# Order of the loads and of the closing products in a LoRA-conditioned routed feed-forward kernel

## The chip, the cores and the metric

The kernel runs on one core of one Trainium2 chip. The metric is the device time of one execution in microseconds, the median of several runs. All data are float32.

## What is computed

Cut to what matters, the reference is this (SCALING of the first part is 2, of the second 1; E is 8 experts, R is 16):

```python
base = einsum('bti,oi->bto', x, W) + b                      # x: 8 x 512 x 2048, W: 2048 x 2048
lora = einsum('btr,bro->bto', einsum('bti,bir->btr', x, lora_As[itok]), lora_Bs[itok])
c = base + 2 * lora                                         # never needed in full
logits = einsum('bsd,ed->bse', c, route_w)                  # 8 logits per token
top, e = top_k(logits, 1)                                   # one expert per token
h = einsum('bsd,erd->bser', c, A)                           # 8 x 16 head values per token
out = x + einsum('bser,eor->bso', one_hot(e) * top * h, Bw)
```

The token's 128 head values and 8 logits are linear in c, and c is linear in x. So the kernel never forms c: it first multiplies W into the 136 columns of A and route_w ("folds" W), and then each tile of 128 tokens needs one product with the folded matrix, a small correction for bias and adapters, the choice of the expert, and one product with Bw.

## The kernel before

**First stage, folding.** W is read in 16 chunks of 128 rows (`load_w`, 1 MB each, four buffers), and `proj`, the 136 columns of A and route_w, in pieces (`load_pj`, tile `pj`, 16 chunks of 68 KB). `chunk_w(oc)` copies chunk `oc` into a layout that TensorE can use as weights, half on ScalarE and half on VectorE (L286, tiles `wv`, two buffers for each half), and issues the load of chunk `oc + 4` into the buffer that comes free. `fold_w(oc)` multiplies it into six PSUM banks `pc` (L297); after the last chunk each bank is copied into `cm`, the folded matrix (L307), by ScalarE and VectorE in turn. Each float32 product is two instructions on TensorE. Between the folds lie the smaller jobs: the indirect loads of the batch's adapters on GpSimd's queue (L173, L203), transposing them (`turn_adapters`, `turn(ad_aT, ...)`), the bias (`fold_bias`, `project_bias`, whose result goes to `g4`), and `project_adapters`, whose result goes through DRAM (`g_dram`) back into `g4`. Before all this GpSimd loads `it_i`, the eight adapter numbers, to every partition (L92).

**Second stage, tokens.** There are 32 tiles `t` of 128 tokens; two tiles are one x unit of 2 MB (`load_x(u)`, L123). To have x with its columns on the partitions, a unit is first moved in 16 blocks of 32 x 1024 (`shuffle`, L254, on GpSimd and ScalarE, tile `xq`), and then VectorE transposes within blocks (`turn_x`, L239, tile `xT`). The main loop takes half a tile per step `n`:

- `heads(t, j0, j1)`, L409: products of xT with `cm` into the PSUM bank `ph`;
- `turn_low(t)`, L421 and L428, on VectorE: the 16 adapter values of the tile, spread and transposed into `hT`; then `add_low(t)`, L433, adds their product with `g4` to `ph`;
- `route(t)`, L446 to L454, on VectorE: five small operations that choose the expert and leave the weighted head values `wh`;
- `turn_heads(t)`, L464, transposes `wh` on TensorE into `pw`, `keep_heads(t)`, L469, copies it to `whT` on ScalarE;
- `delta(t, h)`, L479: the product of whT with 1024 columns of `fb` (Bw) into two banks `po`; `add_delta(t, h)`, L499, adds it to x in place on VectorE, and `store`, L510, writes the result.

`piece(n)` says which half tile is at its `delta` in step n: three steps after its heads. The tiles are written in the order in which each engine shall work (a hand-made order, `manual_schedule`); each engine takes its instructions in that order, and waits stand only where data or buffers ask for them. The queue of SyncE (SP) issues almost all loads and stores. [...]two in `ps_s`, six in `ps_c` for the fold, which afterwards become two in `ps_h` (for `ph`) and four in `ps_o` (for `po`).

The order at the very start, on SP's queue but for the first line:

```python
load_pj(0, 1, nc.scalar)
load_w(0)
load_pj(1, 3)
load_w(1)
load_pj(3, 5)
```

Of the kernel before, what the change touches and what calls it, by code (L numbers as in the profile page):

```python
# [9 lines left out]
F32 = mybir.dt.float32  # L10
# [8 lines left out]
def kernel(  # L19
# [29 lines left out]
    nc = tc.nc  # L49
    P = 128  # L50
    Q = 32
    NQ = P // Q
    B, T, D = x.shape
# [4 lines left out]
    R = ER // E  # L58
    NJ = D // P
# [3 lines left out]
    NT = B * TPB  # L63
# [3 lines left out]
    HJ = NJ // 2  # L67
    HN = D // 512 // 2
    NA = NP + R
# [10 lines left out]
    ps_s = ctx.enter_context(tc.tile_pool(name="ps_s", bufs=2, space=bass.MemoryType.PSUM))  # L80
# [15 lines left out]
    def load_pj(c0, c1, eng=nc.sync):  # L96
        eng.dma_start(out=pj[:, c0:c1, :], in_=proj_v[:, c0:c1, :])
# [3 lines left out]
    def load_w(oc):  # L101
        wt = wpool.tile([P, D], F32, tag="w", bufs=4, name=f"w_{oc}")
        nc.sync.dma_start(out=wt, in_=w[ts(oc, P), :])  # L103
        w_tiles.append(wt)

    load_pj(0, 1, nc.scalar)
    load_w(0)
    load_pj(1, 3)
    load_w(1)
    load_pj(3, 5)  # L110
    load_w(2)
# [3 lines left out]
    x_tiles = {}  # L115
# [3 lines left out]
    def load_x(u):  # L119
        xt = xpools[u % XB].tile([P, TPU, D], F32, tag=f"x{u % XB}", name=f"x_{u}")  # L120
        for k in range(TPU):
            b, r = divmod(TPU * u + k, TPB)
            nc.sync.dma_start(out=xt[:, k, :], in_=x[b, ts(r, P), :])  # L123
        x_tiles[u] = xt
# [3 lines left out]
    make_identity(nc, ident)  # L128

    nc.scalar.copy(warm_a[:, 1:2], warm_a[:, :1])  # L130
    pm = ps_s.tile([P, P], F32, tag="s", name="pm")
    for _ in range(14):
        nc.tensor.matmul(pm, warm, warm, start=True, stop=True)
# [24 lines left out]
    fb = const.tile([P, D], F32, name="fb")  # L158
# [71 lines left out]
    cm = const.tile([P, NJ, NA + R], F32, name="cm")  # L230
    ad_aT = const.tile([P, NJ, P], F32, name="ad_aT")
# [13 lines left out]
    moves = [(g, i) for i in range(NQ) for g in range(NQ)]  # L245

    def shuffle(u, ms, copy):

        if not ms:
            return  # L250
        if u not in xq_tiles:
            xq_tiles[u] = qpool.tile([P, TPU, NQ, DQ], F32, tag="q", name=f"xq_{u}")
        for g, i in ms:
            copy(xq_tiles[u][ts(i, Q), :, g, :], x_tiles[u][ts(g, Q), :, ts(i, DQ)])  # L254
# [66 lines left out]
    def turn_adapters(g):  # L321
        pt = ps_s.tile([P, 4, P], F32, tag="s", name=f"pbT_{g}")
        for k in range(4):
            nc.tensor.transpose(pt[:, k, :], ad_b[:, ts(4 * g + k, P)], ident)  # L324
        nc.scalar.copy(ad_bT[:, ts(g, 4), :], pt)
# [4 lines left out]
    def project_bias():  # L330

        pb = ps_s.tile([P, NP], F32, tag="s", name="pb")
        nc.tensor.matmul(
            pb, one.rearrange("p i s -> p (i s)"), bp, start=True, stop=True
        )
        nc.vector.tensor_copy(g4, pb.unsqueeze(1).to_broadcast([P, B, NP]))
# [16 lines left out]
    for oc in range(NO):  # L353
        if oc + 1 < NO:
            chunk_w(oc + 1)
        fold_w(oc)
        if oc == 2:
            fill_constants()
        if oc == 4:
            load_adapters_b()  # L360
        if oc == 7:
            load_adapters_a()
        if 8 <= oc < 12:
            turn_adapters(oc - 8)
        if oc in (9, 10):
            fold_bias(range(8 * (oc - 9), 8 * (oc - 8)))
        if oc == 10:
            load_x(0)
            nc.sync.dma_start(out=fb, in_=ffn_b)
            load_x(1)  # L370
            load_x(2)
        if oc in (10, 11):
            turn(ad_aT, ad_ar, oc - 10)
        if oc == 11:
            project_bias()
        if oc == 12:
            project_adapters()
            shuffle(0, moves[6:], nc.gpsimd.tensor_copy)
        if oc in (12, 13, 14):
            shuffle(0, moves[2 * (oc - 12) : 2 * (oc - 11)], nc.scalar.copy)  # L380
        if oc == 13:
            for b in range(2):
                nc.vector.tensor_copy(cm[:, :, ds(b * NA, R)], ad_aT[:, :, ts(b, R)])
        if oc == 14:
            for h in range(2):
                turn_x(0, h)
    wctx.close()
    ps_h = ctx.enter_context(tc.tile_pool(name="ps_h", bufs=2, space=bass.MemoryType.PSUM))
    ps_o = ctx.enter_context(tc.tile_pool(name="ps_o", bufs=2, space=bass.MemoryType.PSUM))
# [8 lines left out]
    whT_tiles = {}  # L398
    po_tiles = {}

    def batch_of(t):
        return t // TPB

    def heads(t, j0, j1):
        s = batch_of(t) % 2
        if j0 == 0:
            ph_tiles[t] = ps_h.tile([P, 512], F32, tag="h", name=f"ph_{t}")[:, :NA]
        for j in range(j0, j1):
            nc.tensor.matmul(  # L409
                ph_tiles[t],  # L410
                xT_tiles[t][:, j, :],
                cm[:, j, ds(s * R, NA)],
                start=(j == 0),
                stop=(j == NJ - 1),
            )
# [15 lines left out]
    def add_low(t):  # L431
        b = batch_of(t)
        nc.tensor.matmul(  # L433
            ph_tiles[t][:, ds((1 - b % 2) * R, NP)],
            hT_tiles.pop(t),
            g4[:, b, :],
            start=False,
            stop=True,
            skip_group_check=True,
        )  # L440
# [21 lines left out]
    def turn_heads(t):  # L462
        pw = ps_s.tile([P, P], F32, tag="s", name=f"pw_{t}")
        nc.tensor.transpose(pw, wh_tiles.pop(t), ident)  # L464
        pw_tiles[t] = pw
# [2 lines left out]
        whT_tiles[t] = small.tile([P, P], F32, tag="whT", name=f"whT_{t}")  # L468
        nc.scalar.copy(whT_tiles[t], pw_tiles.pop(t))  # L469

    def delta(t, h):

        if (t, h) == (NT - 1, 0):

            po = [ps_h.tile([P, 512], F32, tag="h", name=f"po_{t}_{k}") for k in range(HN)]
        else:
            po = ps_o.tile([P, HN, 512], F32, tag="o", name=f"po_{t}_{h}")
        for k in range(HN):
            nc.tensor.matmul(  # L479
                po[k] if isinstance(po, list) else po[:, k, :],  # L480
                whT_tiles[t],
                fb[:, ts(h * HN + k, 512)],
                start=True,
                stop=True,
            )
        po_tiles[t, h] = po

    def add_delta(t, h):
        u, k = divmod(t, TPU)
        po = po_tiles.pop((t, h))  # L490
        if t < NT - 1:
            parts = [po.rearrange("p n d -> p (n d)")]
        else:
            parts = po if isinstance(po, list) else [po[:, m, :] for m in range(HN)]
        n = D // 2 // len(parts)
        for m, part in enumerate(parts):
            cols = ds(h * D // 2 + m * n, n)
            xs = x_tiles[u][:, k, cols]
            nc.vector.tensor_tensor(xs, xs, part, ALU.add)  # L499
            if t == NT - 1:  # L500
                store(t, cols)
        if t == NT - 2:
            store(t, ts(h, D // 2))
        elif t < NT - 2 and h == 1:
            store(t, ds(0, D))

    def store(t, cols):
        u, k = divmod(t, TPU)
        b, r = divmod(t, TPB)
        nc.sync.dma_start(out=out[b, ts(r, P), cols], in_=x_tiles[u][:, k, cols])  # L510

    def piece(n):

        return divmod(n - 3, 2) if 0 <= n - 3 < 2 * NT else (-1, -1)
# [15 lines left out]
    for n in range(2 * NT + 4):  # L530
        t, h = divmod(n, 2)
        if t < NT:

            if n == 3:
                heads(t, HJ, HJ + HJ // 2)
                turn_heads(0)
                heads(t, HJ + HJ // 2, NJ)
            else:
                heads(t, h * HJ, (h + 1) * HJ)
            if n == 2:  # L540
                add_low(0)
        if h == 0 and 0 < t <= NT:
            route(t - 1)
        tp, hp = piece(n - 1)
        if tp >= 0:
            add_delta(tp, hp)
        turn_x(t + 1, h)
        if h == 1 and 0 < t <= NT:
            keep_heads(t - 1)
        u, ms = shuffle_slot(n)  # L550
        shuffle(u, ms, nc.gpsimd.tensor_copy if n == 2 else nc.scalar.copy)
        if h == 1 and t < NT:
            turn_low(t)
        if piece(n)[0] >= 0:
            delta(*piece(n))
        if h == 1 and 0 < t < NT:
            add_low(t)
        if h == 1 and t < NT:
            b, k = divmod(t, TPB)
            if k == 0 and 0 < b < B - 1:  # L560
                nc.gpsimd.tensor_copy(
                    cm[:, :, ds((b + 1) % 2 * NA, R)], ad_aT[:, :, ts(b + 1, R)]
                )
        if h == 0 and 1 < t <= NT:
            turn_heads(t - 1)
        tq, hq = piece(n - 5)
        u, k = divmod(tq, TPU)
        if tq >= 0 and hq == 1 and k == TPU - 1 and u + XB < NU:
            load_x(u + XB)
# [48 lines left out]
```

## Time and profile before

| | |
|---|---|
| median of 3 runs | 338.23 us (337.25 to 338.35) |
| profiled execution, its own time | 337.22 us |
| span of the profile | 335.4 us, granted TensorE clock 0.996 |
| PE busy | 324.5 us (97%) |
| DVE busy | 233.4 us (70%) |
| ACT busy | 171.1 us (51%) |
| POOL busy | 136.0 us (41%) |
| moved by DMA | 88.8 MB, 265 GB/s on average |

PE is TensorE's stream of matmuls, PEld its weight loads, DVE is VectorE, ACT ScalarE, POOL GpSimd, SP SyncE; a name with a q behind it is the engine's queue. Times in the profile count from the start of the span. A busy share is an average over the whole span; where the work of one engine fills 97% of it, what that engine waited for in the rest is found in its own timeline, in the brackets ahead of each group.

### The profile page before, as it was taken

How to read it: one execution, taken by the hardware profiler on the slowest of the kernel's cores; microseconds unless marked ns; L12 is line 12 of the kernel's file. 1: busy time of each engine (PE TensorE's matmuls, PEld its weight loads, DVE VectorE, ACT ScalarE, POOL GpSimd, SP SyncE). 2: the span in 40 equal slices, each digit the busy share in tenths (PEclk: the TensorE clock that was granted, in tenths of full speed). 3: DMA queues.
4: the chain of work that ended last, by engine and by line, in shares of the span. 5: the costliest groups of instructions: out<-in, count | busy, mean ns of one | idle time of the engine just before them, and what ended most of it. 6: DMA issues, size and time to landing. Idle time of an engine off the chain costs nothing.

```text
span 335.4 us, 5111 instructions
## 1 busy us (share of the span) xinstructions
PE 324.5 (97%) x1966; PEld 260.3 (78%) x1966; DVE 233.4 (70%) x424; ACT 171.1 (51%) x193; POOL 136.0 (41%) x143
## 2 busy tenths in 40 slices
PE   8899999978999999999999999999999999999993
PEld 8799999978777777777777777777777777777751
DVE  1132385555887877787878787877888777777754
ACT  3233133854857566576647565757575664830000
POOL 2001400899981807182616354344718080800000
PEclk9999999999999999999999999999999999999998
DMA  7999999959233394949485766758494949333336
GB/s 217 402 405 422 416 408 422 419 199 386 117 128 141 132 377 186 376 160 385 136 365 168 335 215 285 256 248 328 174 374 172 374 165 380 164 125 127 126 125 250
DMA packets 15655, 88.82 MB, mean 265 GB/s; under 512 B 1664, under 2 KB 4368, under 8 KB 5392
## 3 DMA queue, kind: packets, MB, share of 16 engines
q1 hardware_dynamic: 14960, 86.33, 65.5%
q0 software_dynamic: 528, 2.11, 2.0%
q8 instruction: 15, 0.25, 0.3%
q10 hardware_dynamic: 144, 0.07, 0.1%
q14 instruction: 8, 0.07, 0.1%
HBM read 54.88 MB, written 33.62 MB: 264 GB/s over the span
## 4 chain that ended last, share of the span: by engine, by line
PE 86%; DMA 6%; POOL 3%; DVE 2%; issue 1%; ACT 1%; SPq 0%; DVEq 0%; POOLq 0%; ACTq 0%
PE ph L409 39%; PE po L479 33%; PE pc L297 10%; DMA x<-in_x_dram 3%; POOL xq L254 3%; DMA w<-in_w_dram 3%; PE ph L433 2%; PE pw L464 1%; DVE xT L239 1%; ACT wv L286 1%; DVE cm L307 0%; PE pbT L324 0%; DVE rw L452 0%; SPq L103 0%; DVE x L499 0%
## 5 line engine op out<-in xcount | busy, mean ns | idle before, releaser
L254 POOL COPY xq<-x 32x1024 f32<-32x1024 f32 x121 | 125.9, 1041 | 122.6 <-DMA x<-in_x_dram 80.7
L254 ACT COPY xq<-x 32x1024 f32<-32x1024 f32 x135 | 140.8, 1043 | 23.8 <-DMA x<-in_x_dram 16.7
L409 PE MATMUL ph<-cm,xT 128*128 128x152 f32 x1024 | 142.7, 293 | 1.8 <-DVE cm L307 1.8
L409 PEld LDWEIGHTS ph<-cm,xT 128*128 128x128 f32 x1024 | 135.2, 190 | 10.6 <-issue 10.6
L479 PE MATMUL po<-fb,whT 128*128 128x512 f32 x256 | 120.2, 592 | 0.4 <-ACT whT L469 0.4
L499 DVE TENSOR_TENSOR x<-x,po 128x1024 f32<-128x1024 f32 (+1 forms) x66 | 77.5, 1178 | 6.6 <-PE po L479 6.2
L239 DVE STREAM_TRANSPOSE xT<-xq 128x1024 f32<-128x1024 f32 x64 | 78.8, 1234 | 4.2 <-POOL xq L254 4.2
L479 PEld LDWEIGHTS po<-fb,whT 128*128 128x128 f32 x256 | 44.8, 190 | 31.8 <-issue 30.9
L297 PE MATMUL pc<-pj,wv 128*128 128x136 f32 x512 | 60.7, 279 | 1.7 <-ACT wv L286 1.6
L297 PEld LDWEIGHTS pc<-pj,wv 128*128 128x128 f32 x512 | 59.8, 190 | 2.1 <-ACT wv L286 1.8
L469 ACT COPY whT<-pw 128x128 f32<-128x128 f32 x32 | 8.5, 266 | 89.7 <-PE pw L464 89.7
L446 DVE TENSOR_REDUCE top<-ph 128x1 f32<-128x8 f32 x32 | 5.3, 167 | 39.0 <-PE ph L433 39.0
L286 DVE COPY wv<-w 128x1024 f32<-128x1024 f32 (+1 forms) x17 | 12.6, 745 | 28.2 <-DMA w<-in_w_dram 16.5
L286 ACT COPY wv<-w 128x1024 f32<-128x1024 f32 (+1 forms) x17 | 16.8, 996 | 24.9 <-DMA w<-in_w_dram 23.4
L433 PEld LDWEIGHTS ph<-g,hT 128*128 128x128 f32 x64 | 12.1, 190 | 14.8 <-issue 12.6
L452 DVE TENSOR_SCALAR rw<-rank,win,top 128x8 f32<-128x8 f32 x32 | 15.6, 488 | 1.2
L433 PE MATMUL ph<-g,hT 128*128 128x136 f32 x64 | 12.6, 279 | 0.0
L464 PEld LDWEIGHTS pw<-ident,wh 128*128 128x128 f32 x32 | 4.5, 140 | 8.7 <-issue 5.7
L428 DVE STREAM_TRANSPOSE hT<-hls 128x128 f32<-128x128 f32 x32 | 10.0, 311 | 1.1
L173 POOL DMA_INDIRECT raw<-in_cond_b_dram,brow_i x1 | 1.0, 1031 | 23.5 <-DVE brow_i L172 23.5
L454 DVE TENSOR_TENSOR wh<-ph,rw 128x128 f32<-128x128 f32 x32 | 9.3, 292 | 1.1
L464 PE MATMUL pw<-ident,wh 128*128 128x128 f32 x32 | 8.8, 274 | 0.8 <-DVE wh L454 0.8
(61 smaller groups left out, 73.5 us busy)
## 6 DMA issues: line engine op xcount, KB each, us to landing
x<-in_x_dram SPq DMA_DIRECT2D x32, 1024.0 KB, 9.0
out_dram<-x SPq DMA_DIRECT2D x30, 1024.0 KB, 4.9
w<-in_w_dram SPq DMA_DIRECT2D x16, 1024.0 KB, 11.2
fb<-in_ffn_b_dram SPq DMA_DIRECT2D x1, 1024.0 KB, 13.1
out_dram<-x SPq DMA_DIRECT2D x2, 512.0 KB, 2.7
out_dram<-x SPq DMA_DIRECT2D x4, 256.0 KB, 2.9
pj<-in_proj_dram SPq DMA_DIRECT2D x2, 272.0 KB, 12.7
pj<-in_proj_dram SPq DMA_DIRECT2D x2, 136.0 KB, 8.0
```

The costliest lines, as they stand in the source:

```text
L239: nc.vector.transpose(dst[:, ts(h, HJ), :].rearrange("p j (g t) -> p g j t", t=Q), src.rearrange("p g (j a) -> p g j a", a=Q)[:, :, ts(h, ...
L254: copy(xq_tiles[u][ts(i, Q), :, g, :], x_tiles[u][ts(g, Q), :, ts(i, DQ)])
L286: copy(dst[:, ts(k, n)], wr[:, ds(h * HJ + k * n, n)])
L297: nc.tensor.matmul(pc[:, k, :], wv_tiles[oc, h][:, j, :], pj[:, oc, :], start=(oc == 0 and k == 0), stop=(oc == NO - 1), skip_group_check= ...
L409: nc.tensor.matmul(ph_tiles[t], xT_tiles[t][:, j, :], cm[:, j, ds(s * R, NA)], start=(j == 0), stop=(j == NJ - 1),)
L428: nc.vector.transpose(hT, h.rearrange("p g s -> p (g s)"))
L433: nc.tensor.matmul(ph_tiles[t][:, ds((1 - b % 2) * R, NP)], hT_tiles.pop(t), g4[:, b, :], start=False, stop=True, skip_group_check=True,)
L452: nc.vector.tensor_scalar(rw, rank, win, top, ALU.is_equal, ALU.mult)
L454: nc.vector.tensor_tensor(wh.rearrange("p (e r) -> p e r", r=R), ph[:, :ER].rearrange("p (e r) -> p e r", r=R), rw.unsqueeze(2).to_broadca ...
L464: nc.tensor.transpose(pw, wh_tiles.pop(t), ident)
L479: nc.tensor.matmul(po[k] if isinstance(po, list) else po[:, k, :], whT_tiles[t], fb[:, ts(h * HN + k, 512)], start=True, stop=True,)
L499: nc.vector.tensor_tensor(xs, xs, part, ALU.add)
```

## The change

Four edits, all of them of order and placing; the computation is the same.

- At the start, W's second chunk is issued directly behind the first on SP's queue. The piece of `proj` for chunks 1 and 2, which stood between them, is issued on ScalarE's queue, after ScalarE's first small copy.
- The first x unit is loaded after fold 8 instead of fold 10, which puts it ahead of the loads of the last two W chunks on SP's queue (14 and 15). Its ten GpSimd blocks are written right behind it. `fb` and x units 1 and 2 are issued one fold later in the text, behind the same W load as before. `project_bias` comes ahead of the second adapter transpose, and the two copies of adapters into `cm` (L383) after fold 11 instead of fold 13.
- In step 2, `add_low(0)` stands in the middle of the half tile's heads instead of behind them.
- In the last two steps that have a `delta` of tile 30, `add_low(31)` and `turn_heads(31)` go in between the two products of that delta. The last tile's results lie in separate banks: two of 512 columns for its first half, and 512, 256 and 256 for the second, each with its own add and its own store; every second store of that tile is issued on ScalarE's queue.

```diff
     load_pj(0, 1, nc.scalar)
     load_w(0)
-    load_pj(1, 3)
     load_w(1)
...
     nc.scalar.copy(warm_a[:, 1:2], warm_a[:, :1])
+    load_pj(1, 3, nc.scalar)
...
-        if oc == 10:
+        if oc == 8:
             load_x(0)
+            shuffle(0, moves[6:], nc.gpsimd.tensor_copy)
+        if oc == 11:
             nc.sync.dma_start(out=fb, in_=ffn_b)
             load_x(1)
             load_x(2)
+            project_bias()
         if oc in (10, 11):
             turn(ad_aT, ad_ar, oc - 10)
         if oc == 11:
-            project_bias()
+            for b in range(2):
+                nc.vector.tensor_copy(cm[:, :, ds(b * NA, R)], ad_aT[:, :, ts(b, R)])
         if oc == 12:
             project_adapters()
-            shuffle(0, moves[6:], nc.gpsimd.tensor_copy)
         if oc in (12, 13, 14):
             shuffle(0, moves[2 * (oc - 12) : 2 * (oc - 11)], nc.scalar.copy)
-        if oc == 13:
-            for b in range(2):
-                nc.vector.tensor_copy(cm[:, :, ds(b * NA, R)], ad_aT[:, :, ts(b, R)])
...
-    def delta(t, h):
+    def delta(t, h, within=None):
...
+            if h == 0:
+                cuts = [bank(ps_h, "h", 512), bank(ps_h, "h", 512)]
+            else:
+                cuts = [bank(ps_o, "o", 512), bank(ps_o, "o", 256), bank(ps_s, "s", 256)]
+            adds = []
+        c = c0
+        for n, part in cuts:
+            nc.tensor.matmul(part, whT_tiles[t], fb[:, ds(c, n)], start=True, stop=True)
+            if t == NT - 1:
+                adds.append((ds(c, n), part))
+            c += n
+            if within:
+                within()
+                within = None
+        po_tiles[t, h] = adds
...
+        for m, (cols, part) in enumerate(po_tiles.pop((t, h))):
             xs = x_tiles[u][:, k, cols]
             nc.vector.tensor_tensor(xs, xs, part, ALU.add)
             if t == NT - 1:
-                store(t, cols)
+                store(t, cols, nc.scalar if m % 2 else nc.sync)
...
+            heads(t, h * HJ, h * HJ + HJ // 2)
             if n == 2:
                 add_low(0)
+            if n == 3:
+                turn_heads(0)
+            heads(t, h * HJ + HJ // 2, (h + 1) * HJ)
...
-        if piece(n)[0] >= 0:
+        last = n in (2 * NT - 1, 2 * NT)
+        if last:
+
+            delta(*piece(n), (lambda: add_low(t)) if h else (lambda: turn_heads(t - 1)))
+        elif piece(n)[0] >= 0:
             delta(*piece(n))
-        if h == 1 and 0 < t < NT:
+        if h == 1 and 0 < t < NT and not last:
             add_low(t)
...
-        if h == 0 and 1 < t <= NT:
+        if h == 0 and 1 < t <= NT and not last:
             turn_heads(t - 1)
```

More of the change, by code (lines that the diff above doesn't have):

```diff
@@ L469, in keep_heads, with bank @@
         nc.scalar.copy(whT_tiles[t], pw_tiles.pop(t))
-    def delta(t, h):
-        if (t, h) == (NT - 1, 0):
-            po = [ps_h.tile([P, 512], F32, tag="h", name=f"po_{t}_{k}") for k in range(HN)]
-        else:
[L477 to L486, printed above, removed]
+    def delta(t, h, within=None):
+        c0 = h * D // 2
+        if t < NT - 1:
+            po = ps_o.tile([P, HN, 512], F32, tag="o", name=f"po_{t}_{h}")
+            cuts = [(512, po[:, k, :]) for k in range(HN)]
+            adds = [(ds(c0, D // 2), po.rearrange("p n d -> p (n d)"))]
+        else:
+            def bank(pool, tag, n):
+                shape = [P, HN, 512] if tag == "o" else [P, 512]
+                b = pool.tile(shape, F32, tag=tag, name=f"pe_{tag}")
+                return n, (b[:, 0, :] if tag == "o" else b)[:, :n]
+            if h == 0:
[13 more added lines that the diff above has]
+        po_tiles[t, h] = adds
     def add_delta(t, h):
         u, k = divmod(t, TPU)
[L490 to L497, printed above, removed]
+        for m, (cols, part) in enumerate(po_tiles.pop((t, h))):
             xs = x_tiles[u][:, k, cols]
@@ L505, in add_delta, with store @@
             store(t, ds(0, D))
-    def store(t, cols):
+    def store(t, cols, eng=nc.sync):
         u, k = divmod(t, TPU)
         b, r = divmod(t, TPB)
-        nc.sync.dma_start(out=out[b, ts(r, P), cols], in_=x_tiles[u][:, k, cols])
+        eng.dma_start(out=out[b, ts(r, P), cols], in_=x_tiles[u][:, k, cols])
     def piece(n):
@@ L532 @@
         if t < NT:
[L534 to L539, printed above, removed]
+            heads(t, h * HJ, h * HJ + HJ // 2)
             if n == 2:
                 add_low(0)
+            if n == 3:
+                turn_heads(0)
+            heads(t, h * HJ + HJ // 2, (h + 1) * HJ)
         if h == 0 and 0 < t <= NT:
```

## The prediction, made before the changed kernel ran

> **What bounds the kernel now.** I read the page first: span 335.4 us, PE busy 97%, and its large groups hardly wait, so only the places where PE stands still can be won. The timeline of PE alone gives them (columns: start, length, group, and in brackets the idle time before it and its releaser):
>
> ```profile
> 6.31 3.97 PE L297 MATMUL pc<-pj,wv 128*128 128x136 f32 x32
> 11.85 29.92 PE L297 MATMUL pc<-pj,wv 128*128 128x136 f32 x256 [1.56 <-ACT wv L286]
> ...
> 75.19 6.44 PE L409 MATMUL ph<-cm,xT 128*128 128x152 f32 x48 [1.78 <-DVE cm L307]
> ...
> 83.73 0.33 PE L464 MATMUL pw<-ident,wh 128*128 128x128 f32 x1 [0.84 <-DVE wh L454]
> ...
> 326.58 3.70 PE L479 MATMUL po<-fb,whT 128*128 128x512 f32 x8 [0.41 <-ACT whT L469]
> ```
>
> Four holes, 1.56 + 1.78 + 0.84 + 0.41 = 4.6 us; after PE ends at 330.28 another 5.1 us follow. The chain that ended last says what filled the second hole (start, length, what):
>
> ```profile
> 48.82 11.04 DMA x<-in_x_dram
> ...
> 71.51 2.37 DVE xT L239 x2
> 73.88 1.17 DVE cm L307 x3
> ```
>
> The first x unit lands at 59.9, POOL shuffles until 71.5, DVE turns the first tile, and three copies of pc queue behind that turn; PE had finished folding at 73.41. The table of windows for the start (window, its length, busy time of PE, PEld, DVE, ACT, POOL; then clock, DMA share, GB/s) shows why W's second chunk is late:
>
> ```profile
> 4.00:5.00 1.00, 1.00 (x7) 1.00 (x7) 0.00 (x0) 0.00 (x0) 0.00 (x0) 1.00 1.02 419
> 5.00:6.00 1.00, 1.00 (x11) 0.99 (x9) 0.17 (x1) 0.17 (x1) 0.00 (x0) 1.00 1.69 117
> 6.00:7.00 1.00, 0.87 (x8) 0.69 (x7) 0.59 (x2) 0.96 (x2) 0.00 (x0) 1.00 0.27 79
> 7.00:8.00 1.00, 1.00 (x11) 1.00 (x10) 0.00 (x0) 0.00 (x0) 0.00 (x0) 1.00 1.01 375
> ```
>
> Two microseconds almost without traffic. The end on DVE, from its timeline:
>
> ```profile
> 330.32 1.28 DVE L499 TENSOR_TENSOR x<-x,po 128x512 f32<-128x512 f32 x2 [1.03 <-PE po L479]
> ```
>
> Both last adds start after the last matmul, though the first bank was full 0.86 earlier: the two banks are one tile.
>
> [...]from 3.3 to 5.3 rows of W0 (SP's queue) and of pj chunk 0 (ACT's) alternate one for one in the packet records. [...]DVE's wv copy takes 0.69 us alone and 1.2 to 1.3 beside POOL's shuffles, rw 0.29 and 0.80. [...]The trace has that in DVE's adds of earlier tiles, which run beside PE's heads in other banks, so pieces in banks of their own can be added one by one.
>
> **The change, part by part.**
>
> A, second W chunk. W0 lands at 5.85, pj(1,3) at 1.19 + 7.0 = 8.2, W1 at 10.72; copies of 1.04, then PE. It looks as if pj(1,3) cost 2.3 us. But its packets are 16 per engine of 28 ns, 0.45 us. In the hole lies another load, it_i on POOL's queue: issued at 1.27, landed 6.6 later at 7.9; the packet records show its 16 packets from 5.6 on, 1.3 us each on average and up to 2.0, one on each engine. Nothing in the diff moves it; POOL's two later loads also began 4.3 to 4.5 us after issue, so I take its time as fixed. On ACT's queue pj(1,3) comes behind pj(0,1), whose turns last until W0 ends, and then alternates with W1's 8 rows per engine: 8 of 16 packets go before W1's end. Gain 8 x 28 ns = 0.2 us. Its rest lands some 0.4 after W1, inside the 1.04 copy. Its issue (0.4 us) falls into ACT's idle time before 5.83. Ends: nothing, or, if the hole went too, 1.56, capped: fold 4 starts at 11.85 + 3 x 3.74 = 23.07 and its copies end at 22.27, so 0.8.
>
> B, first x unit. W13 is issued when its buffer is free at 38.8 (DVE's wv copy, 38.10 + 0.69) and lands 11.3 later, 50.1. x0's two loads now follow it: 2.1 MB at 419 GB/s are 5.0 us, so 55.1 instead of 59.9. POOL's ten copies took 11.5 and end at 66.8; ACT's third pair follows W15's copy, to about 67.4; DVE's turn is done at 69.8. Then the pc copies no longer queue: what is left after 73.41 is the last one, 0.28 on DVE (ACT's ends at 73.72), and 0.15 to PE's start, as at 75.04 to 75.19. PE starts at 73.9: **1.3 us** gained; ends 0.6 (some copy or turn late by a microsecond still) and 1.8 (the whole hole).
> What hides the rest: SP issues x0 (0.92 us) before W14, where it waits for a buffer until 43.8 anyway (ACT's wv copy, 42.72 + 1.05). W14 and W15 landed 8.6 and 6.9 after their issue at 43.8 and 47.9; 5.0 later is 57.4 and 59.8; their copies ran at 62.1 and 65.3. fb, x1 and x2 are issued behind the same loads as before. On POOL the ten copies wait behind nothing but the adapter loads, which are issued before; behind them are x1's moves, and x1 lands near 67. On DVE project_bias now comes before the second ad_aT turn and waits for PE's pb until 54.9; behind it queue 1.29 + 1.24 + 2 x 1.14 + W13's half copy 1.2, to 60.9; PE wants that half at 62.13 + 1.87 = 64.0. Cover gone, it would cost what exceeds 3.1 us.
>
> C, add_low(0) in the middle of a half tile. The route of tile 0 starts when add_low ends (81.63) and reaches turn_heads at 83.73: 2.1 us, over 1.03 of heads. Now 2.06 lies over it, so 0.84 shrinks to under 0.1: **0.8 us**. hT must come earlier: hls and its transpose need 0.65 after heads(0), plus hand-overs, under 1.03. With rw at 0.99 (seen at tile 1) 0.2 would be left.
>
> D, the end. add_low(31) goes half a delta (0.86) earlier; hT is ready at 323.0, PE would reach it at 323.09. The route needs 1.48 from add_low's modelled end to wh and has 0.86 + 0.86 of matmuls over it. turn_heads then stands before the last 0.86 of delta(30,1), over which ACT copies whT. So the 0.41 goes, and the little around it: PE ends 0.5 earlier. After PE, instead of two adds of 0.64, one of 256 columns: from 1209 ns for 1024 and 685 for 512, about 1.02 ns per column and 0.16 fixed, 0.42. Saved 1.32 - 0.04 - 0.42 = 0.85. The last store is half as large; I give nothing for it (256 KB took 2.5 to 3.3, 512 KB 2.7) nor for the one extra matmul. Sum **1.35**; ends 0.8 (the store is slower by as much as 3.3 is over 2.6) and 1.7. ACT's stores stand behind nothing.
>
> Sum 0.2 + 1.3 + 0.8 + 1.35 = 3.65. PE is without holes between these places, and the x loads are triggered by stores that move with it, so I let all of it reach the end. The profiled execution took 337.22 (1.8 outside the span): 333.6. It was the shortest of the three runs; from their median, 338.23, **334.6**.
>
> **Rivals.**
> 1. A brings more: the hole vanishes when W1 stands behind W0. For: it begins exactly when W0 ends. Against: it_i's packets. A is 0.8: 334.0.
> 2. B is mostly lost: another arrival sets PE's start. For: g_dram's small store landed 9.9 us after issue, at 72.6, g4's four loads at about 76.7, and add_low(0) moves from 81.5 to about 78.9; 2.2 us are left, and rows like xq that now run beside DVE's copies can stretch (a POOL copy took 1.40). Then A, C and D alone: 335.9, or, C lost too, 336.7.
> 3. It does not do what it says: x0's chain and the ends were covered by other waits; only D's adds remain, about 337.4.
> 4. Slower: pj(1,3), now on ACT's queue, is starved behind SP's deep one. For: pj loads on SP's queue took up to 13.8 us. From 2.65 that is 16.5, so fold 1 starts 4.6 later than now, C and D still gain 2.15, B's hole is gone anyway (1.3): 338.23 + 4.6 - 3.45 = 339.4. It decides from a landing after 15.3. Against: pj(0,1) on that queue landed in 5.3 us beside W0, in turns.
>
> **How the numbers follow.** Forecast 0.6, rival 1 0.13, rival 2 0.16, rival 3 0.06, rival 4 0.05. About 0.3%, 1.0 us, is what a measurement of this kernel can tell from no change: faster takes the first three, 0.89; rival 3's 0.85 us would be no change, 0.06; slower 0.05. The low end of the range sums the best ends (0.8 + 1.8 + 0.84 + 1.7 = 5.1: 333.1) and lets the median fall some tenths, as two of its runs lie 1 us apart: 332.6. The high end takes in rival 2 with C lost: 336.8.
>
> **What would show it.** Right: fold 1 starts near 11.6; PE's first ph at 73.7; no wait at the first pw; last PE end about 3 us earlier, then one add of about 0.42. Wrong: W1 landing near 8.4 (rival 1), fold 1 after 12 with pj as releaser (rival 4), or a wait of PE on g4 or xT after 74 (rival 2).

## The result, and the profile after

The changed kernel takes 334.60 us (median of 5 runs, 334.54 to 334.82), the kernel before 337.48 (336.93 to 338.35): a ratio of 0.9911, 95% interval 0.9892 to 0.9930. The runs of the kernel before fall in two groups about 1 us apart, which the experiments below take up; its profiled execution, at 337.22, is of the shorter group. The spans of the two profiles are 332.8 and 335.4 us, 2.6 apart.

PE's own timeline after the change (start, length, group, idle time before it and its releaser):

```profile
6.31 3.97 PE L297 MATMUL pc<-pj,wv 128*128 128x136 f32 x32 [0.33 <-DVE wv L286]
11.42 29.92 PE L297 MATMUL pc<-pj,wv 128*128 128x136 f32 x256 [1.14 <-ACT wv L286]
...
73.47 5.41 PE L409 MATMUL ph<-cm,xT 128*128 128x152 f32 x40 [0.48 <-DVE cm L307]
...
81.01 0.27 PE L464 MATMUL pw<-ident,wh 128*128 128x128 f32 x1
```

Each product stands there as two matmuls (fold 0 has 16 products, and its group is x32). Fold 1 starts 0.43 earlier, the first ph 1.72 earlier with 0.48 of idle time left, and the first pw no longer waits. The first po, two lines further, starts at 82.15 instead of 84.93, 2.78 earlier, and this lead stays the same over the whole main loop: heads of the last half tile stand at 317.38 instead of 320.16.

The table of windows at the start (columns as above) has its hole still:

```profile
5.00:6.00 1.00, 0.98 (x9) 0.79 (x8) 0.17 (x1) 0.17 (x1) 0.00 (x0) 1.00 2.03 265
6.00:7.00 1.00, 0.69 (x6) 0.69 (x7) 0.59 (x2) 0.97 (x2) 0.00 (x0) 1.00 0.12 34
7.00:8.00 1.00, 1.00 (x11) 1.00 (x10) 0.00 (x0) 0.00 (x0) 0.00 (x0) 1.00 0.87 316
```

The end, on DVE, and then the table of windows there:

```profile
326.08 1.02 DVE L505 TENSOR_TENSOR x<-x,pe_o 128x512 f32<-128x512 f32 x2 [0.16 <-PE pe_o L492]
327.01 0.41 DVE L505 TENSOR_TENSOR x<-x,pe_s 128x256 f32<-128x256 f32 x1
```

```profile
324.00:325.00 1.00, 1.00 (x3) 0.38 (x2) 1.00 (x2) 0.00 (x0) 0.00 (x0) 1.00 0.94 385
325.00:326.00 1.00, 1.00 (x4) 0.50 (x3) 0.92 (x2) 0.00 (x0) 0.00 (x0) 1.00 0.78 320
326.00:327.00 1.00, 0.90 (x5) 0.45 (x3) 0.92 (x2) 0.00 (x0) 0.00 (x0) 1.00 0.97 383
327.00:328.00 1.00, 0.00 (x0) 0.00 (x0) 0.43 (x2) 0.00 (x0) 0.00 (x0) 1.00 1.02 379
328.00:329.00 1.00, 0.00 (x0) 0.00 (x0) 0.00 (x0) 0.00 (x0) 0.00 (x0) 1.00 1.06 334
329.00:330.00 1.00, 0.00 (x0) 0.00 (x0) 0.00 (x0) 0.00 (x0) 0.00 (x0) 1.00 0.93 286
```

The last add ends at 327.42, 4.18 earlier than before (331.60). But the span ends only 2.6 earlier: from the last add to the end it takes 5.4 us instead of 3.8. All engines are done at 327.4, and the DMA engines (share 0.78 to 1.06) work on stores until 330. So the balance of the span is 0.43 (fold 1) + 1.29 (first ph beyond that) + 1.06 (from first ph to first po, 8.68 instead of 9.74) + 1.40 (last tiles to last add) - 1.58 (after the last add) = 2.60.

### The profile page after: what moved, and what is told of

Its sections match the earlier page's. It is cut to its first block, busy times and chain, and to the rows that moved or that the text cites. A ratio compares the mean times of both kernels' runs of the same rounds, so it can differ in the third digit from the quotient of the medians.

```text
span 332.8 us, 5119 instructions
## 1 busy us (share of the span) xinstructions
PE 323.9 (97%) x1968; PEld 260.4 (78%) x1968; DVE 233.7 (70%) x425; ACT 171.0 (51%) x193; POOL 136.3 (41%) x143
## 4 chain that ended last, share of the span: by engine, by line
PE 94%; DMA 3%; DVE 0%; ACT 0%; SPq 0%; issue 0%; DVEq 0%
PE ph L409 40%; PE po L492 32%; PE pc L297 17%; DMA w<-in_w_dram 3%; PE ph L433 2%; PE pg L342 1%; PE pw L464 1%; PE pbT L324 1%; PE pe_h L492 1%; ACT wv L286 0%; DVE x L505 0%; PE pe_o L492 0%; SPq L103 0%; DVEq L622 0%; DVE cm L307 0%
## 5 line engine op out<-in xcount | busy, mean ns | idle before, releaser
L492 PE MATMUL po<-fb,whT 128*128 128x512 f32 x248 | 116.7, 592 | 0.0
L505 DVE TENSOR_TENSOR x<-x,po 128x1024 f32<-128x1024 f32 x62 | 75.0, 1210 | 5.6 <-PE po L492 5.5
L492 PEld LDWEIGHTS po<-fb,whT 128*128 128x128 f32 x248 | 43.2, 190 | 29.2 <-issue 28.9
L286 DVE COPY wv<-w 128x1024 f32<-128x1024 f32 (+1 forms) x17 | 13.5, 799 | 29.9 <-PE pc L297 16.1
```

Of the source, the lines that this page charges most:

```text
L286: copy(dst[:, ts(k, n)], wr[:, ds(h * HJ + k * n, n)])
L492: nc.tensor.matmul(part, whT_tiles[t], fb[:, ds(c, n)], start=True, stop=True)
```

## Experiments

In each edit, lines with a minus are those of the kernel that the text names, lines with a plus those of the experiment. The times of the experiments come from later batches than the 334.60. The kernel before had medians of 337.12 to 337.31 in these batches, so differences of 0.2 us from the 334.60 are not told apart. The granted clock is the share of its full clock rate that PE was given.

### One edit alone, and each edit undone

**A alone, in the kernel before.**

```diff
     load_w(0)
-    load_pj(1, 3)
     load_w(1)
...
     nc.scalar.copy(warm_a[:, 1:2], warm_a[:, :1])
+    load_pj(1, 3, nc.scalar)
```

> The kernel before with edit A alone (W's second chunk directly behind the first, pj(1,3) on ScalarE's queue). Theory: fold 1 starts at about 11.4 as in the changed kernel, 0.4 us earlier than before, but the first ph stays at about 75.2, since the first x unit's chain ends there whatever the folds do: the span stays at 335.4 and the time is within 0.2 us of before. Rival (each edit's gain adds up by itself): 0.4 us faster.

PE's timeline:

```profile
11.53 29.92 PE L297 MATMUL pc<-pj,wv 128*128 128x136 f32 x256 [1.05 <-ACT wv L286]
...
75.43 6.44 PE L409 MATMUL ph<-cm,xT 128*128 128x152 f32 x48 [2.34 <-DVE cm L307]
```

Fold 1 is earlier, the first ph is not: the hole ahead of it has grown from 1.78 to 2.34. The ratio to before is 1.001 (0.9998 to 1.0023). The 22 runs came in two groups, 10 from 336.97 to 337.44 and 12 from 338.32 to 338.63. For the shorter group the theory held: its median is 337.24, and that of the kernel before's shorter group 337.25. The median of all 22, 338.32, is a microsecond above the 337.31 before, because the longer group is larger here; what sets the groups apart comes with the next experiments.

**A undone, in the changed kernel.**

```diff
+    load_pj(1, 3)
     load_w(1)
...
     nc.scalar.copy(warm_a[:, 1:2], warm_a[:, :1])
-    load_pj(1, 3, nc.scalar)
```

> The changed kernel with A undone (pj(1,3) back between the first two W chunks). Theory: fold 1 back at 11.85, and as the x chain no longer ends last, all of it is passed on: first ph at 73.9, span 333.2, 0.4 us slower than the changed kernel. Rival (A is hidden somewhere): no difference.

335.00 us against 334.60, span 333.1; fold 1 at 11.72, first ph at 73.76, no wait added on the way. With A, fold 1 started between 11.35 and 11.53 in the nine profiles that keep it_i and the loads of the change; without it at 11.85, 11.72 and (in a kernel below) 11.99. So A is worth about 0.4 us, and only where B is there. Two of the six runs, 335.53 and 335.70, lie 0.6 above the other four; no trace of one was kept, and without them A would be 0.3.

**B undone, in the changed kernel.**

```diff
-        if oc == 8:
+        if oc == 10:
             load_x(0)
-            shuffle(0, moves[6:], nc.gpsimd.tensor_copy)
-        if oc == 11:
             nc.sync.dma_start(out=fb, in_=ffn_b)
             load_x(1)
             load_x(2)
-            project_bias()
...
         if oc == 11:
-            for b in range(2):
-                nc.vector.tensor_copy(cm[:, :, ds(b * NA, R)], ad_aT[:, :, ts(b, R)])
+            project_bias()
         if oc == 12:
             project_adapters()
+            shuffle(0, moves[6:], nc.gpsimd.tensor_copy)
...
+        if oc == 13:
+            for b in range(2):
+                nc.vector.tensor_copy(cm[:, :, ds(b * NA, R)], ad_aT[:, :, ts(b, R)])
```

> The changed kernel with B undone (first x unit after fold 10 again, with its shuffles, project_bias and the adapter copies where they were). Theory: first ph at about 75.2, so 1.7 us is lost: B's 1.3 and A's 0.4 with it; span 334.5. Rival (edits add up): 1.3 us slower, span 334.1.

The median is 337.78: 3.2 us slower than the changed kernel, far more than both theories said. The runs are in two groups again, 10 from 336.64 to 337.16 (median 336.95) and 12 from 337.78 to 338.10 (median 337.92); the profile is one of the longer. Its timeline and its windows (the column after the busy times is the granted clock of PE):

```profile
75.13 7.08 PE L409 MATMUL ph<-cm,xT 128*128 128x152 f32 x40 [2.08 <-DVE cm L307]
```

```profile
73.00:75.00 2.00, 0.04 (x1) 0.00 (x0) 2.00 (x5) 1.96 (x3) 1.92 (x3) 1.00 0.47 105
75.00:76.00 1.00, 0.87 (x5) 0.90 (x6) 1.00 (x1) 0.99 (x2) 0.96 (x2) 0.77 1.09 175
76.00:77.00 1.00, 1.00 (x6) 1.00 (x5) 1.00 (x2) 0.99 (x2) 0.96 (x2) 0.50 0.65 238
77.00:78.00 1.00, 1.00 (x6) 1.00 (x5) 0.25 (x1) 0.99 (x2) 0.96 (x2) 0.50 0.99 410
78.00:79.00 1.00, 1.00 (x6) 1.00 (x5) 0.00 (x0) 0.63 (x1) 0.96 (x2) 0.53 0.97 393
```

PE stands idle from 73.05 to 75.13. Worked out from the clock column, the cut to a half begins near 75.54, 0.4 us after PE has started again, and lasts 3.4 us. The same 40 matmuls take 7.08 instead of 5.41, so 1.7 us of PE's time is lost. In the listing of all runs the groups differ in mean granted clock in the same way: 0.990 to 0.994 in the longer, 0.996 to 0.999 in the shorter. This is the only kept trace with the cut; for the other executions it is inferred from their mean clock and time. That the hole is the cause is tried further down.

**C undone, in the changed kernel.**

```diff
-            heads(t, h * HJ, h * HJ + HJ // 2)
+            if n == 3:
+                heads(t, HJ, HJ + HJ // 2)
+                turn_heads(0)
+                heads(t, HJ + HJ // 2, NJ)
+            else:
+                heads(t, h * HJ, (h + 1) * HJ)
             if n == 2:
                 add_low(0)
-            if n == 3:
-                turn_heads(0)
-            heads(t, h * HJ + HJ // 2, (h + 1) * HJ)
```

> The changed kernel with C undone (add_low(0) behind the whole half tile's heads). Theory: PE waits for wh at the first pw again; from the changed kernel's stretch between first ph and first po of 8.68 us against 9.74 before, 1.06 us slower, span 333.8. Rival (only the idle time that the profile shows is at stake): 0.84 us.

335.37 us, 0.77 slower; span 333.5. PE waits again, for less time than in the kernel before:

```profile
81.66 0.33 PE L464 MATMUL pw<-ident,wh 128*128 128x128 f32 x1 [0.47 <-DVE wh L454]
```

The first po is at 82.86, 0.71 later than in the changed kernel. The size is nearer the rival's 0.84. The wait itself varies with rw, which took 0.80 in the profile before and 0.43 in this one: 0.37 less, and the wait is 0.37 shorter too.

**D undone, in the changed kernel:** `delta`, `add_delta`, `store` and the main loop's end as before, A, B and C kept.

```diff
-        last = n in (2 * NT - 1, 2 * NT)
-        if last:
-            delta(*piece(n), (lambda: add_low(t)) if h else (lambda: turn_heads(t - 1)))
-        elif piece(n)[0] >= 0:
+        if piece(n)[0] >= 0:
             delta(*piece(n))
-        if h == 1 and 0 < t < NT and not last:
+        if h == 1 and 0 < t < NT:
             add_low(t)
...
-        if h == 0 and 1 < t <= NT and not last:
+        if h == 0 and 1 < t <= NT:
             turn_heads(t - 1)
```

> The changed kernel with D undone (the last products, their banks, adds and stores as before). Theory: PE reaches the last tiles 2.78 us earlier than before, the end then runs as before (last add at 328.8, 3.8 us to the end of the span): span 332.6, about the same as the changed kernel's 332.8, so D as a whole is worth nothing, since its 1.4 us on the engines comes back as stores that land late and a longer close. Rival (D is worth its share of the engines' gain): span 334.2.

334.65 us, the same as the changed kernel's 334.60. D as a whole, though each of its steps worked on PE and DVE, is worth nothing that these runs can tell.

### Where D's 1.4 us went

**Two pieces instead of three.** In the changed kernel:

```diff
-                cuts = [bank(ps_o, "o", 512), bank(ps_o, "o", 256), bank(ps_s, "s", 256)]
+                cuts = [bank(ps_o, "o", 512), bank(ps_o, "o", 512)]
```

> The changed kernel with the last half tile in two banks of 512 columns instead of 512, 256 and 256: one add of 0.69 instead of 0.41 after the last matmul, one store fewer, and no row of 1 KB. Theory (the DMA engines, busy without a pause from 324 on, set the end, and the last store's semaphore stands first in SP's closing list, which costs 0.5 us): last add 0.27 later, its store lands within 3.0 us, close 0.5 shorter: span 332.3. Rival (the end follows the last add): span 333.1.

The last add is longer, as expected:

```profile
326.94 0.69 DVE L505 TENSOR_TENSOR x<-x,pe_o 128x512 f32<-128x512 f32 x1 [0.17 <-PE pe_o L492]
```

and the kernel is 0.7 us faster: 333.90 us (333.85 to 333.94), span 332.1. The last add ends 0.21 later, so the end does not follow it. The size of the pieces is not all of the gain: 0.43 of it is the order of SP's closing waits, which this edit changes too (next experiment), and the last store's packets end 0.13 earlier (330.25 against 330.38).

**One semaphore earlier in the round.** In the changed kernel, x unit 10 in one DMA:

```diff
+        if u == 10:
+            b, r = divmod(u, TPB // TPU)
+            nc.sync.dma_start(
+                out=xt, in_=x[b, ts(r, TPU * P), :].rearrange("(k p) d -> p k d", p=P)
+            )
-        for k in range(TPU):
+        for k in range(TPU if u != 10 else 0):
```

> The changed kernel with x unit 10 loaded by one DMA of 2 MB instead of two of 1 MB, so that each later DMA takes the semaphore one place earlier in the round and the very last store takes the one that SP's closing list has last. Nothing else moves at the end. Theory: the 0.5 us between the last landing and SP's last wait goes: span 332.3. Rival (the waits of the list are hidden by the landing): 332.8.

334.26 us, 0.34 faster (span 332.5). SP's instruction records show why. They close with a list of waits, each for semaphores that the records name for recent DMAs, one wait after another, 0.06 us each where the DMA is long done. In the kernel before, the last store, landed at 334.20, had the last place in that list, and the wait for its semaphore ended at 334.22. In the changed kernel, which has one DMA more, it had the second: SP's wait for it ends at 331.00, and seven more waits for things long done follow, to 331.43. In this experiment it is last again.

**Less to store.** In the changed kernel; 1 MB of the output is not written:

```diff
         if t == NT - 2:
-            store(t, ts(h, D // 2))
+            pass
```

> The changed kernel without the two stores of tile 30 (1 MB of the output is not written). Theory (the last stores wait behind a backlog on the DMA engines): the last store lands in 2.4 us instead of 3.55, and with two DMAs fewer its semaphore is near the list's end, 0.4 us: span 331.3. Rival (rows of 1 KB are slow by themselves): only the list's 0.4: span 332.4.

Span 331.9, between the two. With the list's order as in the one-load kernel, the comparison with that one is the clean one: from the last store's issue to SP's wait for it, 3.6 us there, 2.9 here, 2.6 in the kernel before. So about 0.7 of the last store's delay is backlog of earlier stores. The other 0.3 is left open. Rows of 1 KB are part of it at most: their packets (the profile's records of the pieces of a transfer, here one a row) took 55 ns on average in the changed kernel's tail and those of 2 KB 94, which is, as an estimate from these two means, 0.12 us for the 16 small ones of each engine (256 on 16 engines).

**Added up.** The packet records of the last 2.1 MB, the stores of tiles 30 and 31, account for D. In the profile with D undone the main loop runs 0.23 later; less that, its first packet of these stores starts at 324.87 and its last ends at 330.82. In the changed kernel they are 324.08 and 330.38. So D starts these stores 0.79 earlier, loses 0.35 because they take longer, and 0.43 in the order of the closing waits: nothing is left. The kernel before had DMA engines as busy at its end, in these windows:

```profile
328.00:329.00 1.00, 1.00 (x4) 0.52 (x3) 0.92 (x2) 0.00 (x0) 0.00 (x0) 1.00 0.98 397
329.00:330.00 1.00, 1.00 (x3) 0.21 (x2) 0.29 (x1) 0.00 (x0) 0.00 (x0) 1.00 1.02 414
330.00:331.00 1.00, 0.28 (x1) 0.00 (x0) 0.68 (x2) 0.00 (x0) 0.00 (x0) 1.00 0.94 363
```

### The hole in the traffic at the start

In the changed kernel:

```diff
-    nc.gpsimd.dma_start(out=it_i, in_=itok.to_broadcast([P, B]))
...
         fold_w(oc)
+        if oc == 3:
+            nc.scalar.dma_start(out=it_i, in_=itok.to_broadcast([P, B]))
```

> The changed kernel with the load of it_i taken from GpSimd's queue at the start and issued on ScalarE's queue after fold 3 instead. Theory (the hole in the traffic at 5.6 to 7.5 is it_i's 16 packets, one of which blocks each DMA engine): the hole goes, W's second chunk lands at 8.4 to 8.7 instead of 10.3, fold 1 starts about 10.3 without a wait, and the gain of 1.1 us reaches the first ph (72.4) if the later chunks hold their lead: span 331.7 to 332.0. Rival (the hole is the start-up of a queue, whoever is on it): W1 lands near 10.3 and the span stays at 332.8.

The windows of the start:

```profile
5.00:6.00 1.00, 1.00 (x10) 1.00 (x9) 0.07 (x1) 0.07 (x1) 0.00 (x0) 1.00 1.01 411
6.00:7.00 1.00, 1.00 (x9) 0.84 (x9) 0.69 (x2) 1.00 (x2) 0.00 (x0) 1.00 1.03 428
7.00:8.00 1.00, 1.00 (x11) 1.00 (x10) 0.00 (x0) 0.07 (x1) 0.00 (x0) 1.00 0.88 349
```

The hole is gone: W1 lands 7.5 us after issue, at 8.7, the folds run without a wait, the first ph comes at 72.17, and the kernel takes 333.26 us, 1.3 less than the changed kernel. The rival as it was put, a start-up of whatever queue, is refuted: without it_i's load there, the 1 MB lands about 1.6 us earlier.

Why those 4 KB are so slow is not settled, since the edit changes the load's queue and its time together. On GpSimd's queue at the start it was 16 packets of 256 bytes, 1.36 us each on average in the changed kernel. On ScalarE's queue, at 23 us, the packet records have 128 packets of 32 bytes, 7 to 15 ns each, and the traffic goes on at 377 to 444 GB/s in each half microsecond. First use of GpSimd's queue alone does not do it: here its first packets come near 32 us, 8 KB each, and take 0.31 us like those that follow.

### The idle stretch and the clock

**The hole of the kernel before, filled** with products whose result nobody reads:

```diff
+    pf = ps_s.tile([P, P], F32, tag="s", name="pf")
+    for _ in range(6):
+        nc.tensor.matmul(pf, warm, warm, start=True, stop=True)
     wctx.close()
```

> The kernel before with six products of the constant warm tile (1.3 us of PE) put on PE between the last fold and the first heads, where PE stood idle for 1.8 us; nothing reads their result. Theory (an idle stretch of about 2 us [...]halves the granted clock for the next 2.8 us, in some executions): with the hole filled no execution has it; all stay at the lower of the two values that the kernel before has, 337.2 us, and none near 338.5. Rival (the two values come from the loads): the split stays.

The median stays (ratio 0.9994). Of 14 executions one, at 338.27 us and a clock of 0.991, still looks cut, so "no execution" was too strong. The kernel before looks cut in 20 of the 92 that ran beside all these experiments (clock 0.992 to 0.994, 338.3 to 339.1 us; the others 336.5 to 338.1). One in fourteen against one in five points the way expected, but is too few to settle it. The 2.8 us in the expectation is a misreading; the trace above has 3.4.

**The same six products in the kernel with B undone.**

```diff
         if oc == 14:
             for h in range(2):
                 turn_x(0, h)
+    pf = ps_s.tile([P, P], F32, tag="s", name="pf")
+    for _ in range(6):
+        nc.tensor.matmul(pf, warm, warm, start=True, stop=True)
     wctx.close()
```

> The changed kernel with B undone and the same six products in the hole. Theory: all executions at B-undone's lower value, 336.9 us or below, clock 1.00 at 75 to 79; and PE waits some 0.8 us for hT at add_low(1) near 86, because turn_low(1) stands on DVE behind the turn of tile 2, which waits for x unit 1's shuffles on POOL (they end at 83.3). Rival (B is only the one hole at the first ph): no such wait, 336.2 us.

Here it is settled: none of 20 executions has the cut, where 12 of 22 had it without the fill. The range is 336.52 to 337.20, the shorter group of the kernel with B undone. So the hole brings the cut. The other kernels agree, by mean clock: holes of 2.34 (A alone) and 2.08 (B undone), each as read from one profile, have it in 12 of 22 each, 1.78 (before) in 20 of 92, and the kernels with 0.48 in none of 35, leaving out the one with A undone, where one of six has 0.994.

The profile shows also what B undone costs beside the hole, on DVE and on PE:

```profile
83.46 2.37 DVE L239 STREAM_TRANSPOSE xT<-xq 128x1024 f32<-128x1024 f32 x2 [0.76 <-POOL xq L254]
...
85.76 0.19 DVE L424 TENSOR_TENSOR hls<-ph,own 128x64 f32<-128x64 f32 x1
...
86.35 0.50 PE L436 MATMUL ph<-g,hT 128*128 128x136 f32 x2 [0.48 <-DVE hT L431]
```

POOL's chain of shuffles runs through from unit 0 to unit 1. Where it starts five microseconds later, the turn of tile 2 waits for it, turn_low(1) stands behind that turn on DVE, and PE waits for hT (the weight load of that product stood 1.31 us). From the first po to this product it is 2.37 us instead of the changed kernel's 1.72, so the wait costs 0.65. B moves it away as well.

The hole, 1.66, and this wait, 0.65, make 2.31, and the shorter group of the kernel with B undone lies 2.35 above the changed kernel. In its profile with the cut this wait is not there: of the 1.7 us that the cut takes, 0.65 would have been lost anyway, and the groups lie 1.0 apart.

### The two gains together

The changed kernel with the load of it_i moved and the last half tile in two pieces:

```diff
-    nc.gpsimd.dma_start(out=it_i, in_=itok.to_broadcast([P, B]))
...
         fold_w(oc)
+        if oc == 3:
+            nc.scalar.dma_start(out=it_i, in_=itok.to_broadcast([P, B]))
...
-                cuts = [bank(ps_o, "o", 512), bank(ps_o, "o", 256), bank(ps_s, "s", 256)]
+                cuts = [bank(ps_o, "o", 512), bank(ps_o, "o", 512)]
```

> The changed kernel with both edits that gained: it_i's load after fold 3 on ScalarE's queue, and the last half tile in two banks of 512. Theory (one is at the start, one at the end, and PE is without holes between): they add up, 1.5 and 0.7 us: span 330.6, 332.5 us. Rival (an end that starts earlier meets the same backlog of stores, so part is lost): 331.1, 333.0 us.

332.90 us (332.80 to 333.01), ratio to before 0.9874 (0.9857 to 0.9890), the fastest version of these runs. It lies 0.3 above what the two gains give when added (334.60 - 0.70 - 1.34 = 332.56). The records explain most of it: the last store again took 3.1 us from issue to SP's wait, as with two pieces alone, but with these DMAs its semaphore came first in the closing list, and 0.43 us of waits followed. An order that puts it last was not run.

## Why the prediction was right, and where not

The time on record, 334.6 us, is the measured median, but that is luck: two errors of about 1 us cancelled. The gain forecast was 3.65 us; between the medians of five runs it is 2.88, between the two profiled executions, both without the cut, 2.64. And the median of three that it was taken from, 338.23, is too high by about as much: its two larger values, 338.23 and 338.35, fit the executions with the clock cut (338.3 to 339.1), though their own clocks are not on record. From the profiled execution the prediction had 333.6, and that is 1.0 too low.

**A, forecast 0.2:** 0.4. The cause was right (it_i's packets stand in the hole, and moving pj does nothing about them), as was the rest of pj landing 0.4 after W1. The size was too small by half, and not through the term "8 of 16 packets": in the changed kernel's packet records 162 of pj's 256 packets, 10 of 16 per engine, start before W1's last row, so that the 6 others spare 6 x 28 ns = 0.17. More than half of the 0.4 is unexplained. (In the profile before, it_i's packets start at 5.3 to 5.6, not "from 5.6 on".) Rival 1 asked for the hole to go, and it only goes when it_i moves. Its cap of 0.8 was too low: it took the copies for fold 4 as fixed at 22.27, and with the hole gone they end at 20.90 and no fold waits. Rival 4 (pj starved on ScalarE's queue) fails: it landed at 1.24 + 9.5 = 10.7.

**B, forecast 1.3:** right as an account of the two profiles: the first x unit lands at 55.0 (forecast 55.1), POOL is done at 66.5 (66.8), PE starts after 0.48 of idle time (1.78 - 1.3 = 0.48), and later W chunks and DVE's queue cost nothing. What it lacked is what the hole did besides being a hole: the clock cut that follows it in a part of the executions, and the wait behind unit 1's shuffles. That is why undoing B costs 2.35 us without the cut and 3.3 with it, and not 1.7. Rival 2, g4 arriving late, did not show.

**C, forecast 0.8:** 0.77 by undoing it, with rw at 0.43; 1.06 between the two profiles, where rw took 0.80 in the one before.

**D, forecast 1.35:** on the engines it was 1.40, with PE ending earlier and one short add behind it as described. Pieces in banks of their own were added one by one: the add from 326.08 to 326.77 ran while PE's products go into other banks until 326.90 (in the profile before, 60 of the 66 adds to x overlapped in time with products of heads). The step that failed is "the last store is half as large; I give nothing for it": from issue to the end of SP's wait the half-size store took 3.55 us where the larger one before took 2.6, and the order of the closing waits took another 0.43. The lower end given for D, 0.8, was too high as well; undone, D is 0.05. I had sized the store by the time of one store alone. The right view would have been the DMA share in the last windows, which is 0.94 to 1.02 from 328 to 331 in the profile before already: the stores of the last two tiles end as soon as the DMA engines have moved them (packets from 324.08 to 330.38 after the change, from 324.87 to 330.82 with D undone), so what counts is when the first of them starts and how long they take. With stores issued closer together, the share is 0.78 to 1.06 from 324 to 330, and what the engines gain becomes a queue.

## What to carry to other kernels

Look at what a tail ends on. Here the DMA engines were busy through it (a share of 0.94 to 1.02 from 328 to 331 in the kernel before): D, with its last add 1.40 us earlier, was worth 0.05, the start of the first store in the queue counted for more (0.79 earlier), and cutting the last piece smaller added rows, semaphores and waits, 0.70 us against two pieces. A gap in the traffic is read by asking which small load lies in it, not which one lies next to it in the order: moving the 4 KB that lay in it was worth 1.34 us, moving the 136 KB next to it 0.4. And a wait of TensorE can be worth more than its length: with a hole of 2.08 us, 1.0 us more in the executions with the clock cut.

## What had not been expected of the hardware

- An idle stretch of PE of 2.1 us was followed, 0.4 us after PE had started again, by a granted clock of 0.50 for 3.4 us. One trace shows it; by mean clock and time it was in 12 of 22 executions of that kernel, and in 20 of 92 of the kernel before, with a stretch of 1.8 us. With six products in the stretch, none of 20 executions of that kernel had it. Why only some executions are hit is not shown by these runs.
- A load of 4 KB that gives all partitions the same 32 bytes, issued on GpSimd's queue at the start, took 1.3 us per packet of 256 bytes on average in the kernel before; from 5.7 to 6.1 us, 15 of the 16 packets under way were its own. A packet of 544 bytes took 28 ns. Issued later on ScalarE's queue, the same load was 128 packets of 7 to 15 ns.
- SP's closing waits cost 0.06 us per DMA semaphore, and their order decides whether they lie under the last store or behind it: 0.34 us between two kernels that differ in one earlier load.
